# Scores and values of a two-layer non-local block in four 64x64 tiles of TensorE

## The chip, the cores and the metric

The kernel runs on one core of one Trainium2 chip. A core has TensorE for matmuls (with a weight load before each), VectorE (DVE), ScalarE (ACT), GpSimd (POOL) and SyncE (SP), which each work through their own queue of instructions and wait for one another on semaphores. Matmuls read SBUF and write PSUM; a PSUM bank here is 128 partitions by 512 float32. The metric is the device time of one execution in microseconds (us).

## What is computed

The input x is (4, 128, 96, 96) in float32. Two layers of the same form follow each other, each with its own weights:

```python
g_x = maxpool2(conv1x1(x, g_w, g_b)).reshape(b, CI, -1).transpose(0, 2, 1)
theta_x = conv1x1(x, theta_w, theta_b).reshape(b, CI, -1).transpose(0, 2, 1)
phi_x = maxpool2(conv1x1(x, phi_w, phi_b)).reshape(b, CI, -1)
f = jnp.einsum('bqc,bck->bqk', theta_x, phi_x)
attn = jax.nn.softmax(f, axis=-1)
y = jnp.einsum('bqk,bkc->bqc', attn, g_x)
y = y.transpose(0, 2, 1).reshape(b, CI, H, W)
W_y = conv1x1(y, W_w, W_b)
inv = bn_gamma * jax.lax.rsqrt(bn_var + BN_EPS)
W_y = W_y * inv[None, :, None, None] + (bn_beta - bn_mean * inv)[None, :, None, None]
return W_y + x
```

Per image and layer that is attention of 96 x 96 = 9216 queries over 48 x 48 = 2304 keys, with CI = 64 channels. All of it is float32.

## The kernel before, in words

There are four images and two layers, so eight blocks (`block`, L280). A block first makes its keys and values (`keys_and_values`, L145): phi (64 channels by 2304 keys, held twice, on partitions 0-63 and 64-127) and gT (keys on partitions, in 18 tiles of 128 keys, by 64 channels). Then it goes through the queries in nine pairs of two query tiles of 512 each (`Pair`, L208). `theta` (L197) projects a pair's queries: the first tile's channels lie on partitions 0-63, the second's on 64-127.

Scores (`scores`, L218) are made transposed: keys on partitions, queries along the free dimension. For one tile k of 128 keys there are two matmuls (L221), one per query tile h. Each contracts 64 channels, so it uses 64 rows of TensorE's array and all 128 columns; h = 0 uses the upper 64 rows and h = 1 the lower. Their outputs are the two banks of one PSUM tile `sc` (pool `ps_sc`, two buffers). ScalarE takes the exponential of both banks at once with a constant shift (L226), and VectorE adds the result to a running sum (L230, L232), from which the softmax denominators come.

Values (`values`, L234) contract the 128 keys of tile k: two matmuls (L239), each with all 128 rows and 64 columns, h = 0 on the left columns and h = 1 on the right. Both add into one PSUM bank `av` (pool `ps_av`, two buffers), h on its own 64 partitions, over all 18 key tiles.

At the end of a pair, `denominators` (L244) sums over the keys' partitions with a matmul by ones (L247), takes reciprocals in four pieces (L253), multiplies `av` by them into `y` (L255) and keeps the largest and smallest reciprocal (L256, L257). `project` (L259) multiplies by W in two matmuls (L267) and VectorE adds shift and x (L273). L200, L247 and L267 share the PSUM pool `ps_misc` (two buffers of one bank). theta (L200) and den (L247) are tiles of 128 rows by 64 columns; W_ps (L267) of 64 rows by 128 columns.

Order is set by the loop in `block` (L289): in batches of two key tiles (KB = 2, nine batches a pair), the scores of batch t are issued, then the values of batch t-1. The next pair's theta follows the values of batch 4. A pair's denominators come after the values of the batch after its last, and its project after the scores of three batches later. The framework may still reorder within an engine's queue; with these priorities the steady part follows the loop. A flag from rmax and rmin chooses at the end whether a general version is run; it isn't run here.

PSUM before: `ps_sc` four banks, `ps_av` two, `ps_misc` two.

Of the kernel before, what the change touches and what calls it, by code (L numbers as in the profile page):

```python
# [9 lines left out]
F32 = mybir.dt.float32  # L10
# [4 lines left out]
PSUM = bass.MemoryType.PSUM  # L15

P = 128
B, C, CI, H, W = 4, 128, 64, 96, 96
HW = H * W
NK = (H // 2) * (W // 2)  # L20
QT = 512
NQ = HW // QT
KT = 128
NKT = NK // KT
# [8 lines left out]
PT = 2 * QT  # L33
# [8 lines left out]
def shifted_blocks(ctx: ExitStack, tc: tile.TileContext, x: bass.AP, layers, out: bass.AP, flag):  # L42
# [8 lines left out]

    nc = tc.nc

    const = ctx.enter_context(tc.tile_pool(name="const", bufs=1))
# [2 lines left out]
    kvp = ctx.enter_context(tc.tile_pool(name="kvp", bufs=2))  # L59
    work = ctx.enter_context(tc.tile_pool(name="work", bufs=2))  # L60
    ps_sc = ctx.enter_context(tc.tile_pool(name="ps_sc", bufs=2, space=PSUM))
    ps_av = ctx.enter_context(tc.tile_pool(name="ps_av", bufs=2, space=PSUM))
    ps_misc = ctx.enter_context(tc.tile_pool(name="ps_misc", bufs=2, space=PSUM))

    ident = const.tile([P, P], F32, name="ident")
# [142 lines left out]
    class Pair:  # L208
# [8 lines left out]

        def scores(self, k):  # L218
            ps = ps_sc.tile([P, PT], F32, tag="sc", name=f"sc_{self.name}_{k}")
            for h in range(2):  # L220
                nc.tensor.matmul(  # L221
                    ps[:, ts(h, QT)], lhsT=self.phi[ts(h, CI), ts(k, KT)],
                    rhs=self.th[ts(h, CI), :], start=True, stop=True,
                )
            e = work.tile([P, PT], F32, tag="exp", name=f"exp_{self.name}_{k}", bufs=6)
            nc.scalar.activation(e, ps, AF.Exp, bias=nshift)  # L226
            self.es[k] = e
            if k == 1:
                self.sum = work.tile([P, PT], F32, tag="sum", name=f"sum_{self.name}")
                nc.vector.tensor_add(self.sum, self.es[0], e)  # L230
            elif k > 1:
                nc.vector.tensor_add(self.sum, self.sum, e)  # L232

        def values(self, k):  # L234
            if k == 0:
                self.av = ps_av.tile([P, QT], F32, tag="av", name=f"av_{self.name}")
            e = self.es.pop(k)
            for h in range(2):
                nc.tensor.matmul(  # L239
                    self.av[ts(h, CI), :], lhsT=self.gT[:, k, :], rhs=e[:, ts(h, QT)],  # L240
                    start=(k == 0), stop=(k == NKT - 1),
                )

        def denominators(self):  # L244
            ps = ps_misc.tile([P, QT], F32, tag="misc", name=f"den_{self.name}")
            for h in range(2):
                nc.tensor.matmul(  # L247
                    ps[ts(h, CI), :], lhsT=ones, rhs=self.sum[:, ts(h, QT)],
                    start=True, stop=True,
                )  # L250
            rc = work.tile([P, QT], F32, tag="rc", name=f"rc_{self.name}")
            for i in range(QT // P):
                nc.vector.reciprocal(rc[:, ts(i, P)], ps[:, ts(i, P)])  # L253
            self.y = work.tile([P, QT], F32, tag="y", name=f"y_{self.name}")
            nc.vector.tensor_mul(self.y, self.av, rc)  # L255
            nc.vector.tensor_tensor(rmax, rmax, rc, ALU.max)  # L256
            nc.vector.tensor_tensor(rmin, rmin, rc, ALU.min)  # L257

# [66 lines left out]
    ps = ps_misc.tile([P, QT], F32, tag="misc", name="bad_ps")  # L325
# [271 lines left out]
def nonlocal_blocks(tc: tile.TileContext, x: bass.AP, layers, out: bass.AP):  # L597
    with tc.tile_pool(name="flag", bufs=1) as pool:
        flag = pool.tile([1, 1], I32, name="flag")
        shifted_blocks(tc, x, layers, out, flag)  # L600
        bad = tc.nc.values_load(flag[0:1, 0:1])
        with tc.If(bad > 0):
            general_blocks(tc, x, layers, out)
# [30 lines left out]
```

## Time and profile before

| what | value |
|---|---|
| median of 3 runs | 2915.18 us (2915.01 to 2915.45) |
| the profiled execution | 2915.95 us, span 2913.7 us |
| granted TensorE clock | 0.993 |
| PE busy | 2842.7 us, 98% of the span |
| DVE busy | 2071.7 us, 71% |
| ACT busy | 1467.4 us, 50% |
| DMA | 14 GB/s on average |

PE is TensorE's matmuls and PEld its weight loads, which overlap them; DVE is VectorE, ACT is ScalarE. The span runs from the first instruction to the last of the profiled execution, and the execution's own time lies a little above it. In rows of groups, a name such as `sc<-theta,phi` says which tile is written from which, `64*128` after it is the part of the array (rows by columns), then the moving operand's shape, the count, and after the bar busy time, mean duration in ns, and the idle time before, with what ended it. L221 is line 221 of the kernel. A matmul's end in the trace is modelled, and records of matmuls on different tiles overlap: starts say more than ends. One float32 matmul of the program leaves two matmul records and two load records.

### The profile page before, as it was taken

Reading aid. Unit: us, or ns where it says so; the run is one execution under the profiler, and the core shown is the slowest. Engines: PE = TensorE matmul, PEld = TensorE weight load, DVE = VectorE, ACT = ScalarE, POOL = GpSimd, SP = SyncE. Lnnn points to the kernel's source line nnn. Section 1 sums busy time; section 2 is a strip of 40 time slices with the busy share of each in tenths; the row PEclk is TensorE's granted clock in tenths of the full one; section 3 lists DMA queues with packets and bytes.
Section 4 is the critical chain, followed back from the end, with each engine's and each line's share of the span. In section 5 each row is a group of like instructions: output and inputs, shape, how many; then the busy total and the mean of one; then the engine's idle time right before and its main releaser. Section 6 shows DMA issues by size and latency. Waiting matters only on the chain.

```text
span 2913.7 us, 29776 instructions
## 1 busy us (share of the span) xinstructions
PE 2842.7 (98%) x11768; PEld 913.5 (31%) x11768; DVE 2071.7 (71%) x2131; ACT 1467.4 (50%) x1420; POOL 1.6 (0%) x8
## 2 busy tenths in 40 slices
PE   7999999999999999999999999999999999999998
PEld 2333333333333333333333333333333333333332
DVE  4777767777677776777767777677776777767776
ACT  3555535555355553555545555455544555445554
POOL 0000000000000000000000000000000000000000
PEclk9999999999999999999999999999999999999999
DMA  3000000000100000000010000000000000000000
GB/s 135 1 1 1 1 1 15 15 15 15 73 1 1 1 1 0 15 15 15 15 73 1 1 1 0 1 15 15 15 15 8 1 0 1 1 0 15 15 15 23
DMA packets 11604, 40.06 MB, mean 14 GB/s; under 512 B 3393, under 2 KB 3777, under 8 KB 11457
## 3 DMA queue, kind: packets, MB, share of 16 engines
q1 hardware_dynamic: 8640, 37.75, 3.3%
q8 instruction: 94, 1.54, 0.2%
q10 hardware_dynamic: 2816, 0.34, 0.1%
q14 instruction: 54, 0.43, 0.0%
HBM read 19.21 MB, written 18.87 MB: 13 GB/s over the span
## 4 chain that ended last, share of the span: by engine, by line
PE 95%; DVE 2%; ACT 1%; DMA 1%; issue 0%; ACTq 0%
PE sc L221 42%; PE av L239 41%; PE gphi_ps L156 4%; PE theta_ps L200 2%; PE W_ps L267 2%; PE den L247 2%; DVE rc L253 1%; DVE gphi L159 1%; PE gT_ps L179 1%; DMA theta_b<-in_L_conv_theta_b_dram 0%; ACT exp L226 0%; DVE centre L169 0%; ACT phi L173 0%; DMA W_nat<-in_L_conv_W_w_dram 0%; ACT phi L176 0%; DMA theta_nat<-in_L_conv_theta_w_dram 0%
## 5 line engine op out<-in xcount | busy, mean ns | idle before, releaser
L226 ACT ACTIVATE exp<-sc,nshift 128x1024 f32<-128x1024 f32 x1296 | 1372.5, 1110 | 1083.7 <-PE sc L221 1083.5
L232 DVE TENSOR_TENSOR sum<-sum,exp 128x1024 f32<-128x1024 f32 x1152 | 1406.3, 1221 | 556.6 <-ACT exp L226 492.2
L221 PE MATMUL sc<-theta,phi 64*128 64x512 f32 x5184 | 1289.0, 615 | 12.6 <-ACT exp L226 8.0
L239 PE MATMUL av<-exp,gT 128*64 128x512 f32 x5184 | 1253.5, 605 | 0.0
L221 PEld LDWEIGHTS sc<-theta,phi 64*128 64x128 f32 x5184 | 445.3, 186 | 840.3 <-issue 457.3
L239 PEld LDWEIGHTS av<-exp,gT 128*64 128x64 f32 x5184 | 315.0, 136 | 859.8 <-issue 853.7
L253 DVE RECIPROCAL rc<-den 128x128 f32<-128x128 f32 x288 | 243.7, 908 | 12.8 <-PE den L247 12.8
L230 DVE TENSOR_TENSOR sum<-exp,exp 128x1024 f32<-128x1024 f32 x72 | 88.2, 1225 | 175.7 <-ACT exp L226 175.7
L156 PE MATMUL gphi_ps<-x,gphiT 128*128 128x384 f32 x384 | 170.5, 556 | 35.6 <-DVE gphi L159 30.5
L159 DVE TENSOR_REDUCE gphi<-gphi_ps 128x96 f32<-128x384 f32 x192 | 105.5, 554 | 62.7 <-PE gphi_ps L156 57.5
L205 ACT ACTIVATE theta<-theta_ps,theta_b 128x512 f32<-128x512 f32 x72 | 49.5, 687 | 150.1 <-PE theta_ps L200 150.1
L173 ACT ACTIVATE phi<-gphi,centre 64x768 f32<-64x768 f32 x24 | 22.3, 930 | 172.1 <-DVE centre L170 136.1
L156 PEld LDWEIGHTS gphi_ps<-x,gphiT 128*128 128x128 f32 x384 | 66.4, 202 | 101.3 <-DVE gphi L159 56.3
L200 PE MATMUL theta_ps<-x,thetaT 128*64 128x512 f32 x288 | 84.0, 595 | 0.0
L267 PE MATMUL W_ps<-y,WT 64*128 64x512 f32 x288 | 77.2, 614 | 4.2 <-DVE y L255 4.2
L247 PE MATMUL den<-sum,ones 128*64 128x512 f32 x288 | 74.0, 592 | 0.0
L273 DVE SCALAR_TENSOR_TENSOR x<-W_ps,shift,x 128x512 f32<-128x512 f32 x72 | 53.6, 744 | 2.7 <-PE W_ps L267 2.7
L273 DVE SCALAR_TENSOR_TENSOR out<-W_ps,shift,x 128x512 f32<-128x512 f32 x72 | 53.5, 744 | 0.8 <-PE W_ps L267 0.8
L257 DVE TENSOR_TENSOR rmin<-rmin,rc 128x512 f32<-128x512 f32 x72 | 49.3, 684 | 0.0
L256 DVE TENSOR_TENSOR rmax<-rmax,rc 128x512 f32<-128x512 f32 x72 | 49.0, 681 | 0.0
L255 DVE TENSOR_TENSOR y<-av,rc 128x512 f32<-128x512 f32 x72 | 48.7, 677 | 0.0
L267 PEld LDWEIGHTS W_ps<-y,WT 64*128 64x128 f32 x288 | 27.4, 188 | 39.1 <-issue 15.8
(45 smaller groups left out, 144.2 us busy)
## 6 DMA issues: line engine op xcount, KB each, us to landing
x<-in_x_dram SPq DMA_DIRECT2D x24, 768.0 KB, 7.5
out_dram<-out SPq DMA_DIRECT2D x36, 512.0 KB, 2.6
theta_nat<-in_L_conv_theta_w_dram ACTq DMA_DIRECT2D x2, 32.0 KB, 5.4
theta_b<-in_L_conv_theta_b_dram ACTq DMA_DIRECT2D x4, 0.2 KB, 6.1
gphi_nat<-in_L_conv_g_w_dram ACTq DMA_DIRECT2D x2, 32.0 KB, 5.6
gphi_nat<-in_L_conv_phi_w_dram ACTq DMA_DIRECT2D x2, 32.0 KB, 5.2
g_b<-in_L_conv_g_b_dram ACTq DMA_DIRECT2D x2, 32.0 KB, 5.5
W_nat<-in_L_conv_W_w_dram ACTq DMA_DIRECT2D x2, 32.0 KB, 5.9
```

What stands on the lines that cost most here:

```text
L156: nc.tensor.matmul(ps[:, :CC], lhsT=w["gphi"], rhs=xt[:, ts(r, CC)], start=True, stop=True)
L159: nc.vector.tensor_reduce(gphi[:, ts(r, CC // 4)].rearrange("p (h w) -> p h w", w=W // 2), ps[:, :CC].rearrange("p (h a w b) -> p h w a b" ...
L200: nc.tensor.matmul(ps[ts(h, CI), :], lhsT=w["theta"], rhs=xt[:, ts(2 * p + h, QT)], start=True, stop=True,)
L221: nc.tensor.matmul(ps[:, ts(h, QT)], lhsT=self.phi[ts(h, CI), ts(k, KT)], rhs=self.th[ts(h, CI), :], start=True, stop=True,)
L226: nc.scalar.activation(e, ps, AF.Exp, bias=nshift)
L230: nc.vector.tensor_add(self.sum, self.es[0], e)
L232: nc.vector.tensor_add(self.sum, self.sum, e)
L239: nc.tensor.matmul(self.av[ts(h, CI), :], lhsT=self.gT[:, k, :], rhs=e[:, ts(h, QT)], start=(k == 0), stop=(k == NKT - 1),)
L247: nc.tensor.matmul(ps[ts(h, CI), :], lhsT=ones, rhs=self.sum[:, ts(h, QT)], start=True, stop=True,)
L253: nc.vector.reciprocal(rc[:, ts(i, P)], ps[:, ts(i, P)])
L267: nc.tensor.matmul(ps, lhsT=self.w["W"][ts(h, CI), :], rhs=self.y[ts(h, CI), :], start=True, stop=True,)
L273: nc.vector.scalar_tensor_tensor(dst[:, ts(h, QT)], pss[h], self.w["shift"], self.xt[:, ts(2 * self.p + h, QT)], op0=ALU.add, op1=ALU.add,)
```

## The change

In `scores`, each of the two matmuls per key tile becomes two, of 64 keys each: the key tile is halved over the columns of the array, and the four matmuls (c, h) are 64 rows by 64 columns each. In `values`, each of the two becomes two as well, halved over the rows: the lower and the upper 64 keys of a tile are contracted by different matmuls (r, h), again 64 by 64, and write to different banks. So `av` becomes two banks, one partial sum per half of the keys, and its pool gets one buffer in place of two, so that it keeps its two banks. After the last key tile ScalarE copies both banks to SBUF (`halves`), and `denominators` adds the two halves before the product by the reciprocals.

```diff
-    ps_av = ctx.enter_context(tc.tile_pool(name="ps_av", bufs=2, space=PSUM))
+    ps_av = ctx.enter_context(tc.tile_pool(name="ps_av", bufs=1, space=PSUM))
...
         def scores(self, k):
             ps = ps_sc.tile([P, PT], F32, tag="sc", name=f"sc_{self.name}_{k}")
-            for h in range(2):
-                nc.tensor.matmul(
-                    ps[:, ts(h, QT)], lhsT=self.phi[ts(h, CI), ts(k, KT)],
-                    rhs=self.th[ts(h, CI), :], start=True, stop=True,
-                )
+            for c in range(2):
+                for h in range(2):
+                    nc.tensor.matmul(
+                        ps[ts(c, CI), ts(h, QT)], lhsT=self.phi[ts(h, CI), ts(2 * k + c, CI)],
+                        rhs=self.th[ts(h, CI), :], start=True, stop=True,
+                    )
...
         def values(self, k):
             if k == 0:
-                self.av = ps_av.tile([P, QT], F32, tag="av", name=f"av_{self.name}")
+                self.av = ps_av.tile([P, PT], F32, tag="av", name=f"av_{self.name}")
             e = self.es.pop(k)
             for h in range(2):
-                nc.tensor.matmul(
-                    self.av[ts(h, CI), :], lhsT=self.gT[:, k, :], rhs=e[:, ts(h, QT)],
-                    start=(k == 0), stop=(k == NKT - 1),
-                )
+                for r in range(2):
+                    nc.tensor.matmul(
+                        self.av[ts(h, CI), ts(r, QT)], lhsT=self.gT[ts(r, CI), k, :],
+                        rhs=e[ts(r, CI), ts(h, QT)],
+                        start=(k == 0), stop=(k == NKT - 1),
+                    )
+            if k == NKT - 1:
+                self.halves = work.tile([P, PT], F32, tag="halves", name=f"halves_{self.name}")
+                nc.scalar.copy(self.halves, self.av)
...
             self.y = work.tile([P, QT], F32, tag="y", name=f"y_{self.name}")
-            nc.vector.tensor_mul(self.y, self.av, rc)
+            nc.vector.tensor_add(self.y, self.halves[:, :QT], self.halves[:, QT:])
+            nc.vector.tensor_mul(self.y, self.y, rc)
```

## The prediction, made before the result was known

> **What bounds the kernel now.** I read the page first: its busy shares and the chain of work that ended last.
>
> ```profile
> PE 2842.7 (98%) x11768; PEld 913.5 (31%) x11768; DVE 2071.7 (71%) x2131; ACT 1467.4 (50%) x1420; POOL 1.6 (0%) x8
> ...
> PE 95%; DVE 2%; ACT 1%; DMA 1%; issue 0%; ACTq 0%
> PE sc L221 42%; PE av L239 41%; PE gphi_ps L156 4%; PE theta_ps L200 2%; PE W_ps L267 2%; PE den L247 2%; DVE rc L253 1%; DVE gphi L159 1%; PE gT_ps L179 1%; DMA theta_b<-in_L_conv_theta_b_dram 0%; ACT exp L226 0%; DVE centre L169 0%; ACT phi L173 0%; DMA W_nat<-in_L_conv_W_w_dram 0%; ACT phi L176 0%; DMA theta_nat<-in_L_conv_theta_w_dram 0%
> ```
>
> TensorE is the bound, and 83% of the chain is the two lines that change. Next the waits of TensorE: does anything else hold it up?
>
> ```profile
> PE gphi_ps L156 <- DVE gphi L159: 30.5, 22, 2.4
> PE sc L221 <- ACT exp L226: 8.0, 8, 1.3
> ```
>
> Hardly: 30 us at the eight block ends, 8 us at block starts. So a gain must come out of TensorE's own time, and I looked for waste inside it. The chain in order of time, where columns are start, length and records, shows the rhythm:
>
> ```profile
> 1004.34 0.86 PE W_ps L267 x4
> ...
> 1011.70 1.92 PE sc L221 x8
> 1013.62 1.87 PE av L239 x8
> ...
> 1026.84 1.92 PE sc L221 x8
> ```
>
> Every matmul leaves two records (L221: 5184 for 2592 in the program). W_ps runs in the tile form of the scores before it, so it joins without a seam: four records in 0.86 us, two steps of 0.43, each step two tiles side by side. Eight records should then take 1.72 us. They take 1.92 (scores) and 1.87 (values). A batch of both costs (1026.84 - 1011.70)/4 = 3.785 us. The timeline at the end of a block, where two batches of values follow each other, gives the step exactly:
>
> ```profile
> 373.47 3.65 PE L239 MATMUL av<-exp,gT 128*64 128x512 f32 x16
> ...
> 376.95 1.03 PE L247 MATMUL den<-sum,ones 128*64 128x512 f32 x4
> ```
>
> Start to start it is 3.48 us for eight steps and one entry, no seam in the middle. The durations of single records (minimum, median, maximum) price the entry:
>
> ```profile
> L221 PEld LDWEIGHTS sc<-theta,phi x5184: 182/186/187, 47.5 to 2894.0; 64*128 64x128 f32 x200
> L221 PE MATMUL sc<-theta,phi x5184: 589/589/693, 47.5 to 2894.4; 64*128 64x512 f32 x200
> ...
> L239 PEld LDWEIGHTS av<-exp,gT x5184: 132/137/137, 53.9 to 2897.6; 128*64 128x64 f32 x200
> L239 PE MATMUL av<-exp,gT x5184: 592/592/643, 53.9 to 2898.0; 128*64 128x512 f32 x200
> ```
>
> The longer ones are the first of a batch, which stand exposed behind their weight load: 693 - 589 = 0.104 us for 128-column weights, 643 - 592 = 0.051 us for 64 columns. The step is (3.48 - 0.05)/8 = 0.429 us. The rest of a seam is a drain: 1.92 - 4 x 0.429 - 0.104 = 0.10 us, and as much at the other. So a batch is eight steps, 3.43 us, and 3.785 - 3.43 = 0.355 us lost at two changes of tile form (64x128 to 128x64 and back).
>
> **The change part by part.**
>
> *Seams removed.* Scores and values both become 64x64 tiles, one form throughout. The array stays as full: two 64x128, two 128x64 and four 64x64 tiles all cover it, and 512 columns still pass per record. Before, two tiles of a step run together whether they differ in rows (scores) or in columns (values); I assume four that differ in both do too. Four matmuls per key tile then need two steps, as now, and the seam goes: 8 blocks x 9 pairs x 9 batches = 648 batches x 0.355 = **-230 us**.
>
> *Seams added.* theta_ps (L200), den (L247) and W_ps (L267) keep their old forms. Today each stands beside a neighbour of its own form; afterwards each is entered and left. Entering W_ps: 0.10 drain + 0.104 load = 0.20; leaving it, and entering or leaving the others, 0.10 + 0.051 = 0.15. Per pair 0.20 + 5 x 0.15 = 0.95 us, x 72 pairs = **+68 us**. No row shows a 64x64 neighbour; bounds are 0 and six times 0.20, 0 to 86 us.
>
> *Weight loads.* Matmul and load records double in number, 10368 each per line. The timeline of a batch of values shows where loads lie now:
>
> ```profile
> 988.27 1.94 PE L239 MATMUL av<-exp,gT 128*64 128x512 f32 x8
> 988.75 0.14 PEld L239 LDWEIGHTS av<-exp,gT 128*64 128x64 f32 x2 [0.29 <-issue]
> 989.18 0.14 PEld L239 LDWEIGHTS av<-exp,gT 128*64 128x64 f32 x2 [0.28 <-issue]
> ```
>
> The second step starts at 988.27 + 0.05 + 0.43 = 988.75, and with it the two loads for the third, side by side; they are done long before 989.18. I expect four to lie there as two do: **0**, unless TensorE can't issue that fast (rival 1).
>
> The two value tiles share all 128 rows, and yet only a batch's first load is exposed. The Trainium skill, "TensorE: Matmul & The Clock Gate", Part 3, The mechanism, says that a load overlaps matmuls in flight only where the row group differs. By that rule the new tiles that share rows would show a load at every step (rival 3); these rows speak against it.
>
> *The copy on ScalarE (new).* 128x1024 out of PSUM, once per pair. Nearest rows:
>
> ```profile
> L226 ACT ACTIVATE exp<-sc,nshift 128x1024 f32<-128x1024 f32 x1296 | 1372.5, 1110 | 1083.7 <-PE sc L221 1083.5
> ...
> L205 ACT ACTIVATE theta<-theta_ps,theta_b 128x512 f32<-128x512 f32 x72 | 49.5, 687 | 150.1 <-PE theta_ps L200 150.1
> ```
>
> 1.11 us by exp, the same shape; at most 2 x 0.687 = 1.37. ScalarE goes to 1467 + 80 = 1547 us, not a bound. But `ps_av` loses its second buffer, so the next pair's first values wait for this copy. Between the two stand the scores of one batch, four steps, 1.72 us. An exp starts some 0.22 us after its scores have streamed:
>
> ```profile
> 990.13 1.99 PE L221 MATMUL sc<-theta,phi 64*128 64x512 f32 x8
> ...
> 991.31 2.12 ACT L226 ACTIVATE exp<-sc,nshift 128x1024 f32<-128x1024 f32 x2 [1.67 <-PE sc L221]
> ```
>
> (990.13 + 0.10 + two steps = 991.09; start 991.31.) The copy is thus done 0.22 + 1.11 = 1.33 us after the values, 0.39 before they are wanted again, and with 1.37 still 0.13 before. Behind it in ScalarE's queue is the next exp, 0.25 us late, whose values are a batch away. I take **0**; without that cover every 0.1 us costs 72 x 0.1 = 7 us.
>
> *The add on VectorE (new).* 128x512, same shape as rmax:
>
> ```profile
> L256 DVE TENSOR_TENSOR rmax<-rmax,rc 128x512 f32<-128x512 f32 x72 | 49.0, 681 | 0.0
> L255 DVE TENSOR_TENSOR y<-av,rc 128x512 f32<-128x512 f32 x72 | 48.7, 677 | 0.0
> ```
>
> 0.68 us; the product, now out of SBUF, stays at 0.68. VectorE goes to 2072 + 49 = 2121 of some 2757 us, 77%. At a pair's end it runs behind, so I checked who waits:
>
> ```profile
> 999.31 0.68 DVE L255 TENSOR_TENSOR y<-av,rc 128x512 f32<-128x512 f32 x1
> ...
> 1004.17 1.02 PE L267 MATMUL W_ps<-y,WT 64*128 64x512 f32 x4
> ...
> 1006.23 0.74 DVE L273 SCALAR_TENSOR_TENSOR x<-W_ps,shift,x 128x512 f32<-128x512 f32 x1
> ...
> 1010.68 1.03 PE L200 MATMUL theta_ps<-x,thetaT 128*64 128x512 f32 x4
> ```
>
> y has 4.2 us to spare before W_ps, and the first W_ps bank is read out 3.7 us before theta_ps needs it. The add takes 0.68 of each and TensorE, ahead by under four seams, at most 1.4. Both keep over 1.6 us: **0**. At a block's end nothing covers the add:
>
> ```profile
> 381.75 0.67 DVE L255 TENSOR_TENSOR y<-av,rc 128x512 f32<-128x512 f32 x1
> ...
> 382.73 0.30 PEld L267 LDWEIGHTS W_ps<-y,WT 64*128 64x128 f32 x4 [0.55 <-DVE y L255]
> ```
>
> Eight times 0.68 = **+5 us**.
>
> *Sum* against the profiled execution: 2913.7 - 230 + 68 + 5 = 2757 us of span; it ran 2915.95, 2.3 outside the span, and lies 0.8 above the median 2915.18. Forecast **2758 us**, its own range 2690 (added seams free) to 2800 (dearest seams, copy cover partly lost).
>
> **The rivals.**
>
> *1. TensorE's issue becomes the bound (slower).* A step now holds 8 instructions (four loads, four matmuls) where it held 4: one each 53.6 ns instead of 107. Nothing in this kernel runs long at that pace. The densest rows are two transposes in a row:
>
> ```profile
> 397.05 0.33 PE L179 MATMUL gT_ps<-ident,gphi 64*128 64x64 f32 x2
> ...
> L179 PE MATMUL gT_ps<-ident,gphi x144: 222/271/366, 28.4 to 2569.5; 64*128 64x64 f32 x144
> ```
>
> The second matmul starts 0.33 - 0.222 = 0.11 us after the first with a load between: 55 to 56 ns an instruction, which may be the array's work rather than issue. So the price lies between 53.6 or less (free) and 107 (nothing faster shown for long). A batch has 64 instructions: each ns above 53.6 costs 64 x 648 = 41.5 us. The net gain of 157 us is gone at 57.4 ns: that is where it decides. At 56 it gives 2758 + 100 = **2858**; a tenth above the densest row, 61.6 ns (my choice, near that row), gives 2758 + 332 = **3090 us**. Against it: "issue 0%" in the chain, but at half the pace.
>
> The same page of the Trainium skill, Part 2, phase 2, gives about 62 ns per matmul when microcode decodes it, and names no figure for a load. No run here shows it; matmuls alone would fit (4 x 62 = 248 ns of a 429 ns step, an estimate), with loads as dear it would be 2758 + (62 - 53.6) x 41.5 = 3107.
>
> *2. Four tiles don't run together.* If those that share rows or columns go in turn, each step takes two rounds: 8 x 0.429 x 648 = +2224, **4982 us**. Rows alone and columns alone pair up in the trace; both at once isn't shown. That the change doesn't do what it says is this case.
>
> *3. Weight loads come out from behind the matmuls.* If tiles that share rows wait for their load at every step, 0.051 x 8 steps x 648 = 264: **3022 us**. Against it stand the loads at 988.75 and 989.18, which begin a whole step early.
>
> **How the numbers follow.** Forecast 0.60; rival 1 at its mild end (about 2858) 0.08; a net nil 0.02; rival 1 beyond break-even (about 3090) 0.20; rival 2 0.08; rival 3 0.02. A difference under 0.2% can't be told from none. Faster 0.68, same 0.02, slower 0.30. The range begins at the forecast's lower bound, 2690, and must reach past the break-even into rival 1: to 3100, where half of its slower part is in, 0.60 + 0.08 + 0.02 + 0.10 + 0.02 = 0.82.
>
> **What would show it.** Right: eight records to a step of 0.43 us; scores and values with 10368 records each and almost none longer than their median; a batch of 3.43 us in the chain; theta_ps, den and W_ps entered behind idle loads; one ScalarE copy per pair near 1.1 us, with no TensorE wait for it. Wrong: records of the third and fourth tile starting late in the step (issue), steps of 0.86 (no concurrency), first values of a pair waiting for the copy, or theta_ps waiting for VectorE.

## The result, and the profile after

The changed kernel takes 2764.06 us (median; 2760.82 to 2764.58) against 2915.28, a ratio of 0.9479 with a 95% interval of 0.9463 to 0.9495. The forecast was 2758. The profiled execution has a span of 2762.3 us, 151.4 less than before.

First the page of the changed kernel: busy shares and the costliest groups of the two changed lines, of the copy and of the added sum. (Lines have moved: scores are L223, values L242, the copy L249, den L254, the sum of the halves L262, W_ps L275.)

```profile
PE 2689.1 (97%) x22136; PEld 911.1 (33%) x22136; DVE 2115.4 (77%) x2203; ACT 1536.5 (56%) x1492; POOL 1.6 (0%) x8
...
L223 PE MATMUL sc<-theta,phi 64*64 64x512 f32 x10368 | 1237.4, 592 | 13.0 <-ACT exp L228 8.4
L242 PE MATMUL av<-exp,gT 64*64 64x512 f32 x10368 | 1230.7, 590 | 0.0
...
L249 ACT COPY halves<-av 128x1024 f32<-128x1024 f32 x72 | 72.9, 1012 | 46.4 <-PE av L242 46.4
...
L262 DVE TENSOR_TENSOR y<-halves 128x512 f32<-128x512 f32 x72 | 49.3, 685 | 15.5 <-ACT halves L249 15.5
```

TensorE is still the bound. The records of scores and values have doubled, and their means, 592 and 590 ns, lie next to the 589 of an undisturbed record: hardly any stands behind an exposed load now. And the matmuls of the values never waited (0.0 idle), so the copy, at 1.01 us, stayed within its cover. The timeline at a pair's end shows how much was left:

```profile
1007.76 1.01 ACT L249 COPY halves<-av 128x1024 f32<-128x1024 f32 x1 [0.45 <-PE av L242]
...
1008.83 0.15 PEld L242 LDWEIGHTS av<-exp,gT 64*64 64x64 f32 x4 [0.30 <-ACT halves L249]
1009.23 1.04 PE L242 MATMUL av<-exp,gT 64*64 64x512 f32 x8
```

The copy ends at 1008.77, 0.46 us before the next pair's first values start (0.39 predicted). Their first weight load, however, does wait for it: the copy lets it go about when it would have started anyway, and a load of 0.15 us still fits before the matmul.

The chain in order of time, from the steady part:

```profile
1004.26 1.72 PE sc L223 x16
1005.98 1.72 PE av L242 x16
...
1011.13 1.01 PE den L254 x4
1012.14 1.88 PE sc L223 x16
...
1020.88 1.06 PE W_ps L275 x4
1021.94 1.88 PE av L242 x16
```

Sixteen matmul records take the 1.72 us that eight should have taken before: four to a step of 0.43, and eight with their loads, as the prediction counts them. Two batches take 1011.13 - 1004.26 = 6.87 us, so one takes 3.435 where it took 3.785. What is left of the seams stands around den (1.01 - 0.86 = 0.15 to enter, 1.88 - 1.72 = 0.16 to leave) and W_ps (0.20 and 0.16).

The waits of TensorE show what the block ends became (columns: the sum in us, times, the longest):

```profile
PE W_ps L275 <- DVE y L263: 31.5, 8, 5.2
...
PE gphi_ps L157 <- DVE gphi L160: 5.2, 9, 1.5
```

Together 36.7 us. Before, the waits at the same places were the 30.5 for gphi that the prediction shows and one for y at the very end:

```profile
PE W_ps L267 <- DVE y L255: 4.2, 1, 4.2
```

That makes 34.7, so the waits grew by 2 us. They moved from gphi to y because TensorE's order at a block end changed: W_ps now starts before the next matmuls of gphi (704.11 and 706.12), where gphi came first (381.89 and 382.73).

The block ends themselves grew by more. The view by stretches gives a stretch, its length, busy time by engine, then the granted clock, the DMA share and GB/s. Here each stretch runs from den of a block's last pair to the first scores of the next block. Two block ends before:

```profile
376.95:410.12 33.17, 28.39 (x80) 11.26 (x77) 22.12 (x38) 4.23 (x6) 0.00 (x0) 0.90 0.00 0
738.24:768.91 30.67, 25.89 (x80) 10.51 (x77) 22.05 (x38) 4.23 (x6) 0.00 (x0) 1.00 0.43 171
```

and the same two after:

```profile
356.32:389.67 33.35, 28.63 (x83) 11.74 (x79) 22.82 (x39) 5.24 (x7) 0.00 (x0) 0.90 0.00 0
697.80:731.08 33.28, 28.56 (x83) 11.70 (x79) 22.82 (x39) 5.25 (x7) 0.00 (x0) 0.90 0.40 158
```

Before, four of the seven ends between blocks are like the first row (33.1 to 33.2 us at a clock of 0.90) and three like the second (30.7 us at full clock). After, all seven take 33.2 to 33.4 us at 0.90. Together they took 224.6 us and now take 232.7, 8 more, and 3 x 2.5 = 7.5 of that goes with the clock.

Between two such stretches lies a block's loop: 328.1 us before (410.12 to 738.24) and 308.1 after (389.67 to 697.80), over the eight blocks 160 us less. The prices from the chain give nearly that. A block has eighty changes each way, since its first two batches of scores and its last two of values follow each other: -0.35 x 640 = -224. Eight each of theta_ps, den and W_ps lie inside a block's loop: +(0.31 + 0.31 + 0.36) x 64 = +63 (theta_ps taken like den); sum -161. The whole difference, -151.4, is thus made up: -160 in the loops, +8 at the ends between blocks, and +0.4 ahead of the first scores and behind the last den.

### The profile page after: what moved, and what is told of

Read it like the earlier page. It is cut to its first block, busy times and chain, and to the rows that moved or that the text cites. A ratio compares the mean times of both kernels' runs of the same rounds, so it can differ in the third digit from the quotient of the medians.

```text
span 2762.3 us, 50645 instructions
## 1 busy us (share of the span) xinstructions
PE 2689.1 (97%) x22136; PEld 911.1 (33%) x22136; DVE 2115.4 (77%) x2203; ACT 1536.5 (56%) x1492; POOL 1.6 (0%) x8
## 4 chain that ended last, share of the span: by engine, by line
PE 95%; DVE 2%; ACT 1%; DMA 1%; issue 0%; ACTq 0%
PE av L242 41%; PE sc L223 41%; PE gphi_ps L157 5%; PE W_ps L275 3%; PE theta_ps L201 3%; PE den L254 3%; DVE rc L260 1%; PE gT_ps L180 1%; DVE gphi L160 0%; ACT exp L228 0%; DMA W_nat<-in_L_conv_W_w_dram 0%; DVE centre L170 0%; ACT phi L174 0%; ACT phi L177 0%; DMA theta_b<-in_L_conv_theta_b_dram 0%; DMA theta_nat<-in_L_conv_theta_w_dram 0%
## 5 line engine op out<-in xcount | busy, mean ns | idle before, releaser
L223 PE MATMUL sc<-theta,phi 64*64 64x512 f32 x10368 | 1237.4, 592 | 13.0 <-ACT exp L228 8.4
L242 PE MATMUL av<-exp,gT 64*64 64x512 f32 x10368 | 1230.7, 590 | 0.0
L223 PEld LDWEIGHTS sc<-theta,phi 64*64 64x64 f32 x10368 | 381.6, 133 | 763.2 <-issue 735.7
L242 PEld LDWEIGHTS av<-exp,gT 64*64 64x64 f32 x10368 | 390.0, 133 | 729.2 <-issue 710.2
L260 DVE RECIPROCAL rc<-den 128x128 f32<-128x128 f32 x288 | 243.7, 908 | 12.6 <-PE den L254 12.6
L275 PE MATMUL W_ps<-y,WT 64*128 64x512 f32 x288 | 88.9, 696 | 31.5 <-DVE y L263 31.5
L249 ACT COPY halves<-av 128x1024 f32<-128x1024 f32 x72 | 72.9, 1012 | 46.4 <-PE av L242 46.4
L254 PE MATMUL den<-sum,ones 128*64 128x512 f32 x288 | 77.7, 618 | 0.0
L262 DVE TENSOR_TENSOR y<-halves 128x512 f32<-128x512 f32 x72 | 49.3, 685 | 15.5 <-ACT halves L249 15.5
L275 PEld LDWEIGHTS W_ps<-y,WT 64*128 64x128 f32 x288 | 23.3, 198 | 88.6 <-issue 51.2
```

The lines of the kernel that those rows point to most:

```text
L223: nc.tensor.matmul(ps[ts(c, CI), ts(h, QT)], lhsT=self.phi[ts(h, CI), ts(2 * k + c, CI)], rhs=self.th[ts(h, CI), :], start=True, stop=True,)
L242: nc.tensor.matmul(self.av[ts(h, CI), ts(r, QT)], lhsT=self.gT[ts(r, CI), k, :], rhs=e[ts(r, CI), ts(h, QT)], start=(k == 0), stop=(k == N ...
L254: nc.tensor.matmul(ps[ts(h, CI), :], lhsT=ones, rhs=self.sum[:, ts(h, QT)], start=True, stop=True,)
L275: nc.tensor.matmul(ps, lhsT=self.w["W"][ts(h, CI), :], rhs=self.y[ts(h, CI), :], start=True, stop=True,)
```

## The experiments

The theory on trial: **the gain is the seams**, a price at each change of tile form (by the prediction a drain and an exposed first load), and nothing else; the costs are what the prediction named. Its rivals: small tiles are faster in themselves; TensorE's issue is near its limit; the single buffer or VectorE takes something back. Ratios are to the kernel before, each from runs on the same chip, with 95% intervals.

### One line alone

Scores in four tiles with values, `ps_av` and `denominators` as before:

```diff
...
+                    nc.tensor.matmul(
+                        ps[ts(c, CI), ts(h, QT)], lhsT=self.phi[ts(h, CI), ts(2 * k + c, CI)],
...
```

And the reverse, the new values, `ps_av`, copy and sum with the scores as before:

```diff
...
+                    nc.tensor.matmul(
+                        self.av[ts(h, CI), ts(r, QT)], lhsT=self.gT[ts(r, CI), k, :],
...
```

> Only the scores become four 64x64 tiles; values stay 128x64 in one bank with two buffers, no copy and no added sum. Seam theory (the gain is the drain of 0.10 us and the exposed first load at each change of tile form): scores and values still differ in form, so both changes of a batch stay; entering the scores exposes a 64-column load (0.05) in place of a 128-column one (0.10): -0.053 x 648 = -34 us; W_ps now stands between two foreign forms, +0.20 x 72 = +15. About 2896 us, ratio 0.993. Rival (four smaller tiles are faster in themselves, each converted line bringing half of the gain): 2840 us, ratio 0.974.

> Only the values become four 64x64 tiles, with the copy and the added sum; scores stay 64x128. Seam theory: both changes of a batch stay at their price; theta_ps and den are now entered by a change of their own, 2 x 0.15 x 72 = +22 us; the block ends cost +5 to +10 as in the changed kernel. About 2944 us, ratio 1.010. Rival (four smaller tiles are faster in themselves): 2840 us, ratio 0.974.

Scores alone: 2904.25 us, 0.9972 (0.9961 to 0.9982). Values alone: 2946.18 us, 1.0112 (1.0095 to 1.0129). Neither brings half of the gain; one brings almost nothing and the other costs. The chain in order of time, scores alone:

```profile
1002.16 1.88 PE sc L222 x16
1004.03 1.87 PE av L240 x8
...
1031.11 1.06 PE W_ps L268 x4
```

and values alone:

```profile
1005.95 1.01 PE den L253 x4
1006.96 1.92 PE sc L222 x8
1008.87 1.88 PE av L241 x16
```

The same sixteen records that take 1.72 us in the changed kernel take 1.88 here, since the neighbour has another form. Values alone came within 2 us of the seam theory's 2944. Scores alone gained less than its -19 us: a batch fell by 0.04 us (1.92 to 1.88), not by the 0.053 expected from the load alone, so -26 with +0.20 x 72 = +14 makes -12; the spans of the profiled executions differ by 13.1 (2900.6 against 2913.7), the medians by 9.

### Twice as many seams

```diff
-KB = 2
+KB = 1
...
-                    hooks.setdefault((t + 1, "columns"), []).append(done.denominators)
-                    hooks.setdefault((t + 4, "rows"), []).append(done.project)
+                    hooks.setdefault((t + 2, "columns"), []).append(done.denominators)
+                    hooks.setdefault((t + 8, "rows"), []).append(done.project)
```

> The kernel before with batches of one key tile in place of two, the steps at a pair's end kept at the same distance in key tiles: twice as many changes between scores and values. Seam theory: +648 x 0.355 = +230 us, about 3145 us, ratio 1.079. Rival (a change of form costs nothing of its own; the lost time lies elsewhere in a batch, in proportion to the key tiles): 2915 us, ratio 1.00.

> The changed kernel with batches of one key tile. Seam theory: one tile form throughout the loop, so the number of batches has no price: 2764 us within 15 us, ratio to the kernel before 0.948. Rival (alternating between scores and values costs even in one form, by new PSUM banks or new weights): up to +230 us, 2994 us, ratio 1.027.

In the kernel before: 3146.69 us, 1.0798 (1.078 to 1.0816); the seam theory said 3145. The chain shows each batch of one key tile paying as much as a batch of two did:

```profile
1011.47 1.06 PE sc L221 x4
1012.53 1.01 PE av L239 x4
```

1.06 - 0.86 = 0.20 and 1.01 - 0.86 = 0.15. In the changed kernel: 2807.03 us, 0.9633 (0.9617 to 0.9649), 43 more than the 2764 expected. Alternation itself is free there, as these rows of its chain show, but at a pair's end something new appears:

```profile
1017.19 0.86 PE sc L223 x8
1018.05 0.86 PE av L242 x8
...
1021.55 0.88 ACT exp L228
...
1022.57 1.01 ACT halves L249
...
1023.62 1.09 PE av L242 x8
```

Its waits name it:

```profile
PE av L242 <- ACT halves L249: 26.8, 64, 0.4
PE av L242 <- ACT exp L228: 11.4, 16, 1.3
```

With batches of one, only one key tile of scores (0.86 us) stands between a pair's last values and the next pair's first, and the copy needs more. Each wait shows 0.42 us of idle time; beside it lie the 0.16 us by which a record outlasts its step (0.589 - 0.429) and a freshly exposed load of 0.05: 0.63 x 64 = 40 us. Besides the cover being halved, the copy here starts late, behind an exp in ScalarE's queue. The loops of the eight blocks took 47 us more than in the changed kernel: these 40, and some 3 for exp (11.4 us of waiting here, 8.4 there); the ends between blocks took 6 less. So most of the miss is not a price of alternating; it is the single buffer with its cover gone, which the prediction had priced by the tenth of a microsecond.

### The cover of the single buffer

```diff
-                nc.scalar.copy(self.halves, self.av)
+                nc.vector.tensor_copy(self.halves, self.av)
```

> The changed kernel with the copy of the two halves on VectorE in place of ScalarE. If the one buffer of the values is free only because ScalarE ends the copy 0.3 to 0.4 us ahead: VectorE is in the first sums of the next pair when the values end, the copy (about 1.2 us, by the sum of the same size) ends 2.0 to 2.1 us after them, the next values want their banks after 1.72, so 0.3 to 0.4 us x 72 = 22 to 29 us are lost: 2786 to 2793 us, ratio 0.957. If the wait has cover enough anyway: 2764 us, ratio 0.948.

2793.32 us, 0.9587 (0.9571 to 0.9603): 29 us lost. The chain at a pair's end, and the wait:

```profile
1019.54 1.22 DVE sum L232
1020.76 1.15 DVE halves L249
...
1021.96 1.95 PE av L242 x16
```

```profile
PE av L242 <- DVE halves L249: 21.8, 64, 0.3
```

VectorE takes the copy only after the first sum of the next pair, as expected. That the loss came out at the upper end of the expected 22 to 29 us is partly luck: the expectation counted the waits alone. With the 0.21 us that each wait brings along, as in the run before, 64 of them make (0.34 + 0.21) x 64 = 35 us. The loops took 36 us more than in the changed kernel, and the ends between blocks 6 or 7 less, at a higher clock. The buffer is free in the changed kernel because ScalarE, with time on its hands, empties it early.

### How near TensorE's issue is to its limit

Eight tiles of 64x32 instead of four: the step is the same work in sixteen instructions.

```diff
-            for c in range(2):
+            for c in range(4):
...
-                        ps[ts(c, CI), ts(h, QT)], lhsT=self.phi[ts(h, CI), ts(2 * k + c, CI)],
+                        ps[ts(c, 32), ts(h, QT)], lhsT=self.phi[ts(h, CI), ts(4 * k + c, 32)],
...
-            for h in range(2):
+            for q in range(4):
                 for r in range(2):
                     nc.tensor.matmul(
-                        self.av[ts(h, CI), ts(r, QT)], lhsT=self.gT[ts(r, CI), k, :],
-                        rhs=e[ts(r, CI), ts(h, QT)],
+                        self.av[ts(q, 32), ts(r, QT)], lhsT=self.gT[ts(r, CI), k, ts(q % 2, 32)],
+                        rhs=e[ts(r, CI), ts(q // 2, QT)],
```

> Scores and values in eight tiles of 64 rows by 32 columns, otherwise the changed kernel: 16 instructions of TensorE in a step of 0.429 us, one each 26.8 ns, and 128 in a batch. If TensorE issues one within 26.8 ns for long, the time stays at that of the changed kernel, with shorter loads at the three entries from other forms (-0.025 x 3 x 72 = -5): about 2759 us, ratio 0.947. If issue is the limit, each ns above 26.8 costs 128 x 648 = 83 us: an interval of 40 ns gives 3860 us, and the interval of 53.6 ns that the changed kernel is known to reach gives 4980 us.

2762.91 us, 0.9486 (0.947 to 0.9502): the time of the changed kernel. Its chain (the last row stands behind den) and its group of values:

```profile
1005.36 1.72 PE sc L223 x32
1007.08 1.72 PE av L242 x32
...
1009.80 1.88 PE sc L223 x32
```

```profile
L242 PE MATMUL av<-exp,gT 64*32 64x512 f32 x20736 | 1246.3, 590 | 0.0
```

Thirty-two matmul records in 1.72 us, with as many loads: one instruction each 26.8 ns, through all the loops. The changed kernel needs half that pace. If there is a limit of issue, it is no dearer than that. One thing expected did not come: a first load of 32 columns exposes less (its record is at most 613 ns long, against 640 with 64 columns), but the 5 us are not seen. A block's loop takes 308.1 us as before, and the scores behind den 1.88 us. So the whole price of a seam is shown; its division into a drain and an exposed load is not.

### The seams that are left

W_ps split over its columns, which needs no partial sums:

```diff
-                nc.tensor.matmul(
-                    ps, lhsT=self.w["W"][ts(h, CI), :], rhs=self.y[ts(h, CI), :],
-                    start=True, stop=True,
-                )
+                for c in range(2):
+                    nc.tensor.matmul(
+                        ps[ts(c, CI), :], lhsT=self.w["W"][ts(h, CI), ts(c, CI)],
+                        rhs=self.y[ts(h, CI), :], start=True, stop=True,
+                    )
```

> The changed kernel with W_ps, too, as 64x64 tiles (its 128 columns halved; no partial sums). Seam theory: the two changes of form around W_ps, measured 0.20 + 0.16 us in the changed kernel, are gone: -0.36 x 72 = -26 us, 2738 us, ratio 0.939. Rival (what is left around W_ps is a wait for VectorE or PSUM banks, not its form): 2764 us, ratio 0.948.

2736.84 us, 0.9394 (0.9378 to 0.941): 27 us less than the changed kernel, 26 expected. In the loops the traces show 23 us less, 0.36 x 64; the rest lies at the block ends. In the chain both seams are gone:

```profile
1008.31 1.72 PE sc L223 x16
1010.03 0.86 PE W_ps L276 x8
1010.89 1.72 PE av L242 x16
```

### The block ends

In the changed kernel VectorE's timeline at a block end is longer than the add alone would make it, since rmax comes between the sum of the halves and the product:

```profile
702.23 0.63 DVE L262 TENSOR_TENSOR y<-halves 128x512 f32<-128x512 f32 x1
702.78 0.68 DVE L264 TENSOR_TENSOR rmax<-rmax,rc 128x512 f32<-128x512 f32 x1
703.37 0.68 DVE L263 TENSOR_TENSOR y<-y,rc 128x512 f32<-128x512 f32 x1
```

The sum ahead of the reciprocals:

```diff
         def denominators(self):
+            self.y = work.tile([P, QT], F32, tag="y", name=f"y_{self.name}")
+            nc.vector.tensor_add(self.y, self.halves[:, :QT], self.halves[:, QT:])
...
-            nc.vector.tensor_add(self.y, self.halves[:, :QT], self.halves[:, QT:])
             nc.vector.tensor_mul(self.y, self.y, rc)
```

> The changed kernel with the sum of the halves ahead of the reciprocals in VectorE's queue in place of behind them, where the denominators' matmul hides it. If the block ends pay for the add: y is ready about 0.63 us earlier at eight block ends, -5 us, and if the lower granted clock after the longer idle time goes with it at the ends between images, -8 us more: 2751 to 2759 us, ratio 0.944 to 0.946. If something else sets the block ends: 2764 us, ratio 0.948.

2756.25 us, 0.9463 (0.9447 to 0.9479): 8 us less than the changed kernel, though the two intervals overlap. TensorE's wait at the ends is shorter; its waits now read, beside one of 4.8 us for y at the very end:

```profile
PE gphi_ps L157 <- DVE gphi L160: 25.0, 17, 3.0
```

25.0 + 4.8 = 29.8 against 36.7, 7 us. The stretches of the trace show where the time went. The loops take as long as in the changed kernel (308.1 us a block), and the seven ends between blocks 224.9 us against 232.7: there lie the 8 us. Three of these ends have a granted clock of 0.90, as all seven had, and take 32.6 to 32.9 us in place of 33.2 to 33.4. The other four have 0.95 and take 31.5 to 31.7, as this one:

```profile
1036.90:1068.60 31.70, 27.51 (x82) 10.97 (x78) 22.52 (x39) 5.24 (x7) 0.00 (x0) 0.95 0.00 0
```

A rough split, an estimate from these ends: 0.4 x 7 = 3 us are the early sum at equal clock, and the other 5 go with the higher clock. What sets the clock at an end is not shown. The length of the wait alone does not: before, TensorE waits 2.42 us for gphi at the ends of both kinds, ahead of the matmuls at 381.89 and at 743.17, and one end has a clock of 0.90 and the other the full clock.

Both improvements together:

> W_ps in 64x64 tiles and the sum of the halves ahead of the reciprocals, both together. If the two gains are of different places (a change of form in the loop, VectorE at the block ends) they add: 2764 - 27 - 8 = 2729 us, ratio 0.937. If both come from the same place (W_ps waiting at the block ends): about 2737 us, ratio 0.939.

2727.07 us, 0.9369 (0.9344 to 0.9395): they add (2764 - 27 - 8 = 2729), and this is the fastest version found. On top of it, theta_ps and den over row halves, each in two banks of `ps_misc`:

```diff
+        pss = [ps_misc.tile([P, QT], F32, tag="misc", name=f"theta_ps_{name}_{p}_{r}")
+               for r in range(2)]
...
+                nc.tensor.matmul(
+                    pss[r][ts(h, CI), :], lhsT=w["theta"][ts(r, CI), :],
+                    rhs=xt[ts(r, CI), ts(2 * p + h, QT)], start=True, stop=True,
+                )
...
+        nc.vector.tensor_add(th, th, pss[1])
...
+            nc.scalar.copy(rc, pss[0])
+            nc.vector.tensor_add(rc, rc, pss[1])
```

> The kernel before this one (W_ps in 64x64 tiles, early sum) with theta_ps and den, too, in 64x64 tiles: their 128 rows halved into two banks of the shared pool, joined by one add on VectorE each, with one more copy on ScalarE for den. Seam theory: two times 0.31 us a pair are gone, -0.62 x 72 = -45 us; the added 1.4 us on the way to the reciprocals at eight block ends and 0.7 us at eight block starts cost +17: about 2701 us, ratio 0.927. Rival (VectorE, already behind at a pair's end, or the two shared banks that theta_ps and den now both take, become the bound): each 0.6 us of waiting a pair takes the gain back, 2729 us or more, ratio 0.937 or above.

2765.95 us, 0.9487 (0.947 to 0.9505): 39 us worse than without it. The seam theory's 2701 failed here and the rival held. In the chain of a steady pair VectorE takes the place of TensorE from den to theta_ps:

```profile
858.25 1.22 DVE sum L237
859.47 0.67 DVE x L289
...
860.18 0.65 PE theta_ps L203 x3
```

theta_ps now needs both banks of the shared pool, so it waits for the second x of `project`, and that for VectorE, which works off the sums delayed by den. TensorE's waits for this are short in the page's count:

```profile
PE theta_ps L203 <- DVE out L289: 6.7, 28, 0.6
...
PE theta_ps L203 <- DVE x L289: 5.9, 28, 0.2
```

12.6 us of idle, plus what each wait brings along, where 45 us were to be gained. The traces split the loss. Against the kernel without this step the loops take 6 us more (2449 against 2443 in all), so the 0.62 x 64 = 40 us to be gained inside them are gone. The seven ends between blocks take 258 us against 218, with granted clocks of 0.86 to 0.95 against 0.95 to 1.00. This profiled execution is the slowest of its four, some 10 us above the median. How much of the ends is the longer way to the reciprocals and how much the clock was not tried apart, and stays open.

## Why the prediction was right

**The bound and the waste.** A batch of 3.785 us was read as 3.43 us of streaming and 0.355 of seams. After the change a batch is 3.435. Doubling the seams in the kernel before gave +233 us (3146.69 - 2913.31, the kernel before on that chip) for the +230 worked out (in the traces 240 in the loops, and 6 less at the block ends): the price of a seam is shown from both sides. In the count of seams the prediction is a little off: 81 a block, where the loop has eighty.

**Four tiles together** was the assumption with no row behind it. It held: four matmul records to a step. Rival 2 (4982 us) is out.

**Seams added.** 0.95 us a pair predicted, 0.98 measured (0.15 and 0.16 at den, 0.20 and 0.16 at W_ps); the run with W_ps in 64x64 tiles took W_ps's part away and got it back.

**The copy** at no cost: right, and by the cover that the prediction named, 0.46 us against its 0.39; the copy takes 1.01 us, not 1.11. With the copy moved to a late engine 29 us come back, and with one key tile of scores in its way in place of two, 43.

**The add.** Nothing inside a block, as predicted. For the block ends the prediction said +5 us, and that this is near the measured +8 is luck. At equal clock an end takes 33.1 to 33.2 us before and 33.2 to 33.4 after, so 0.68 us for the add are not seen there. The growth goes with the granted clock, which was full at three of the seven ends before and at none after; the prediction has no term for the clock. Nor did it see that VectorE's queue would put rmax between the sum and the product.

**Rival 1, issue** (0.28 in all) was the main doubt, and it was far off: 53.6 ns an instruction was needed, 26.8 are reached. The densest row quoted, 55 to 56 ns, was no limit of issue. The figure that the Trainium skill, "TensorE: Matmul & The Clock Gate", Part 2, gives for decoding in microcode (about 62 ns a matmul) doesn't describe this chip's run: eight matmuls in a step of 429 ns are one each 54 ns, beside eight loads.

**Rival 3, loads that come out,** is refuted, with the rule of the Trainium skill that the prediction set behind it: tiles that share a row group (the rows of the array that they take) load beside each other's matmuls in all three forms tried (128x64, 64x64, 64x32), with 589 to 592 ns as the usual record.

Of the 6 us between forecast and result, 2 lie in the loops (160 us less, by the prediction's sum 162) and 3 to 4 at the block ends and the two ends of the kernel. So the mechanism of the gain held as told, seam by seam; the term for the block ends was near by luck.

## What to carry to other kernels

Where a loop alternates between two tile forms of TensorE, compare a group's time with its steps: what is over is a price per change, not per work, and a common form removes it, even at twice the instructions. Convert all that alternates or nothing: half the conversion brought 0.3% or cost 1.1%. In this kernel it stopped paying where the common form needed partial sums on an engine that was already behind at the same moment. And check a small term at its own place: the sum can come out right while the clock, and not the term, makes the difference.

## What the runs showed of the hardware that was not expected

TensorE keeps one load or matmul each 26.8 ns (64x32 tiles, 41472 matmul records of scores and values) with no loss against 53.6. The granted clock at a block end is not a matter of the wait's length alone: 0.90 at one end and full at the next, after equal waits of 2.42 us. And tiles need not keep step: in the last kernel one of the four runs a step apart from the other three after a wait, and the batch still takes its time.

```profile
860.85 0.42 PE theta_ps L203 x3
861.27 1.29 PE sc L226 x12
862.56 0.42 PE sc L226 x3
```

Three records of one line share a step with one of the next line; 1.29 + 0.42 = 1.71 us for the scores of a batch, as when all four keep step.
